# Waves of perceptron units in pairs, and outputs at the end of the same step

## The chip, the cores and the metric

The kernel runs on one core of a Trainium2 chip. The metric is the device time of one execution in microseconds (us); less is better. TensorE (PE) does matrix products into PSUM, which has eight banks of 128 partitions x 512 f32. VectorE (DVE) and ScalarE (ACT) read PSUM and write SBUF; SyncE (SP) issues nearly all DMAs; GpSimd (POOL) hardly works in the part that is changed.

## The reference

A chain of four layers on an image batch of shape (4, 16, 512, 512), f32: an attention block, a quantised 3x3 convolution with batch norm and a clip, two 3x3 convolutions with a residual, and a 3x3 convolution followed by a two-layer perceptron over the channels with a residual. The change touches the last three, as they are run in one tail loop. Cut to what matters there:

```
# layer 1
xq, wq = fake_quant(x), fake_quant(weight)
y = conv3x3(xq, wq)
y = y * inv + (beta - mean * inv)          # batch norm over the batch
x = clip(y, 0.0, 6.0)
# layer 2
out = relu(conv3x3(x, w1) + b1)
x = conv3x3(out, w2) + b2 + x
# layer 3, 128 hidden units
y = conv3x3(x, conv_w)
h = relu(einsum('bchw,kc->bkhw', y, w1) + b1)
x = x + einsum('bkhw,ck->bchw', h, w2) + b2
```

## The kernel before

The first part (attention, then a pass that takes the mean and variance for the batch norm) is left as it is. The tail is the last loop of `conv_layers`. It works through 128 tiles (`TP`), each of four image rows: 128 partitions hold rows and channels, and 2 x 512 elements lie along the free dimension. It is a pipeline in steps T. In step T each stage works on another tile:

- `load(T + 3)` (line 941): two DMAs bring the input into a buffer `tx`.
- `quantised(T + 2)`: scaling on VectorE (line 1011), rounding on ScalarE (line 1014), then four DMAs (lines 1065 and 1068) that copy quarters of `qe` into `qo`, the tile shifted by a row.
- `stage_z(T)`: the quantised convolution in bf16; each half goes out of PSUM on its own engine with the batch norm's scale and shift (line 1142 ScalarE, line 1143 VectorE), then one VectorE instruction clips both (line 1144), then four DMAs copy `ze` into `zo`.
- `stage_h(T - 1)`, `stage_x(T - 3)`, `stage_y(T - 4)`: the three f32 convolutions, each through `convolve` (line 1123), each copied out of PSUM by VectorE or ScalarE (lines 1160/1161, 1171, 1182/1183); h and x are also copied into `ho` and `xo` by four DMAs each.
- `wave(T - 6, k)` for k = 0 to 3: four matmuls of the perceptron's first layer (line 1198), one PSUM bank each; four activations into tiles `hid`, in turn on VectorE (line 1208) and ScalarE (line 1206). The function returns the four units.
- `outputs(T - 7, units)`: sixteen matmuls of the second layer over the units of four waves (line 1218), two additions on VectorE (line 1224), and one DMA to the output (line 1227).

The order of instructions on PE, DVE, ACT and SP is the order of the program; it is written out by hand (`manual_schedule`). Every DMA of the tail is in SP's order too. A wait at the head of such an order holds what is behind it.

The stages take PSUM banks from one counter: `take(n)` gives the next n of eight banks in turn. A wave takes four, every convolution two, outputs two; that is 26 in a step. A bank is written again when what it held has been read.

TensorE is split into tiles of another size by stage, which the profile prints as rows*columns: 64*32 for the convolutions, 32*128 for a wave, 128*32 for outputs. An f32 matmul shows as two records.

The kernel prepares and unpacks its arrays on the host; none of this is in the time.

Of the kernel before, what the change touches and what calls it, by code (L numbers as in the profile page):

```python
# [29 lines left out]
TP = H // 4  # L30
NH, HD = 2, 8
WS = 8
T = WS * WS
# [71 lines left out]
def conv_chain(ctx: ExitStack, tc: tile.TileContext, x, xw, mats, vecs, cqs, cws, hots, out):  # L105
# [32 lines left out]
    with tc.If(safe == 0):  # L138
        attention_block(tc, x, x1, m, v, peak)
    conv_layers(tc, x1, out, cw, cq, sw, m, v, peak)  # L140


# [784 lines left out]
def _quad(i):  # L927
    return slice(32 * i, 32 * i + 32)
# [19 lines left out]
def conv_layers(ctx: ExitStack, tc, x1, out, cw, cq, sw, m, v, peak):  # L948
# [13 lines left out]
    def take(n):  # L962
        return [banks[next(turn) % 8] for _ in range(n)]
# [3 lines left out]
    def ring(name, n, dt=F32):  # L967
        tiles = rings[name] = [
            act.tile([P, 2, WP], dt, name=f"{name}{i}") for i in range(n)
        ]  # L970
        return lambda k: tiles[k % n]
# [6 lines left out]
    ze, zo, he, ho = ring("ze", 4), ring("zo", 3), ring("he", 2), ring("ho", 2)  # L978
# [19 lines left out]
    def inner(t):  # L998
        return t[:, :, 1 : W + 1]
# [3 lines left out]
    def load(n, dst=None):  # L1003
        if dst is None:
            dst = ld.tile([P, 2, W], F32, tag="x", name=f"tx{n}")
        loaded[n] = dst
        _load_pairs(nc, dst, x1, n)
# [62 lines left out]
    def quantised(n):  # L1070
        scaled(n)
        rounded(n)
        shift(n, qe, qo, n < TP)
# [39 lines left out]
    def convolve(weights, pair):  # L1113

        p = take(2)
        for dx in range(3):
            for w in range(2):
                if pair[w] is None:
                    continue
                src, odd = pair[w]  # L1120
                for f in range(2):
                    for r in range(2):
                        nc.tensor.matmul(  # L1123
                            p[r][_quad(2 * f + w)], weights[_half(r), odd, dx, :],
                            src[_half(r), f, dx : dx + W],
                            start=dx == 0, stop=dx == 2,
                        )
        return p

    def shift_ends(n, e, o):  # L1130

        shift(n, e, o, ends=True)
        if n == TP - 1:
            for i in (0, 2):
                nc.gpsimd.memset(o(n)[_quad(i)], 0.0)

    def stage_z(n):

        if not 0 <= n < TP:
            return  # L1140
        p, z = convolve(cq, ((qe(n), 0), (qo(n), 1))), inner(ze(n))
        nc.scalar.activation(z[:, 0], p[0], AF.Identity, bias=shift_by, scale=scale)  # L1142
        nc.vector.tensor_scalar(z[:, 1], p[1], scale, shift_by, ALU.mult, ALU.add)
        nc.vector.tensor_scalar(z, z, ACT_MAX, 0.0, ALU.min, ALU.max)  # L1144
        shift_ends(n, ze, zo)

    def stage_h(n):

        if not 0 <= n <= TP:
            return  # L1150
        second = (ze(n), 0) if n < TP else None
        p, h = convolve(cw[:, 0], ((zo(n - 1), 1), second)), inner(he(n))
        if n in (0, TP):
            e = slice(n // TP, n // TP + 1)
            for f in range(2):
                nc.scalar.activation(
                    h[:, f], p[f], AF.Relu, bias=edge_b1[:, e], scale=v("edge")[:, e]
                )
        else:
            nc.scalar.activation(h[:, 0], p[0], AF.Relu, bias=v("l2_b1"))  # L1160
            nc.vector.tensor_scalar(h[:, 1], p[1], v("l2_b1"), 0.0, ALU.add, ALU.max)  # L1161
        shift(n, he, ho, n < TP)

    def stage_x(n):

        if not 0 <= n < TP:
            return
        p = convolve(cw[:, 1], ((he(n), 0), (ho(n), 1)))
        x, z = inner(xe(n)), inner(ze(n))
        for r in range(2):  # L1170
            nc.vector.scalar_tensor_tensor(
                x[:, r], p[r], v("l2_b2"), z[:, r], ALU.add, ALU.add
            )
        shift_ends(n, xe, xo)

    def stage_y(n):

        if not 0 <= n <= TP:
            return
        second = (xe(n), 0) if n < TP else None  # L1180
        p, y = convolve(cw[:, 2], ((xo(n - 1), 1), second)), inner(ye(n))
        nc.scalar.copy(y[:, 0], p[0])
        nc.vector.tensor_copy(y[:, 1], p[1])
# [5 lines left out]
    def wave(n, k):  # L1189

        if not 0 <= n < TP:
            return []
        units, p = [], take(4)
        for q in range(4):
            w, f = divmod((k + q) % 4, 2)
            par = w ^ (q % 2)
            src = ye(n + (w and not q % 2))
            nc.tensor.matmul(  # L1198
                p[q], w1[_quad(q), 1 - par, :], inner(src)[_quad(q), f, :],
                start=True, stop=True,  # L1200
            )
        for q in range(4):
            w, f = divmod((k + q) % 4, 2)
            hd = ld.tile([P, W], F32, tag="hid", name=f"hid{n}_{k}_{q}", bufs=24)
            if next(count) % 2:
                nc.scalar.activation(hd, p[q], AF.Relu, bias=v("l3_b1"))  # L1206
            else:
                nc.vector.tensor_scalar(hd, p[q], v("l3_b1"), 0.0, ALU.add, ALU.max)  # L1208
            units.append((q // 2, 2 * f + w, w ^ (q % 2), hd))
        return units  # L1210

    def outputs(n, units):

        if not units:
            return
        p, o, seen = take(2), inner(xe(n)), set()
        for r, c, par, hd in units:
            nc.tensor.matmul(  # L1218
                p[r][_quad(c)], w2[:, par], hd,
                start=(r, c) not in seen, stop=(r, c) in seen,  # L1220
            )
            seen.add((r, c))
        for r in range(2):
            nc.vector.scalar_tensor_tensor(  # L1224
                o[:, r], p[r], v("l3_b2"), o[:, r], ALU.add, ALU.add
            )
        nc.sync.dma_start(out[n], o)

    units = []
    for T in range(TP + 7):  # L1230
        if T + 3 <= TP:
            load(T + 3)
        outputs(T - 7, units)
        units = wave(T - 6, 0)
        stage_y(T - 4)
        units += wave(T - 6, 1)
        if T + 2 <= TP:
            quantised(T + 2)
        stage_x(T - 3)
        units += wave(T - 6, 2)  # L1240
        stage_h(T - 1)
        stage_z(T)
        units += wave(T - 6, 3)


def _strips(a):
# [127 lines left out]
```

## Time and profile before

| | |
|---|---|
| median of 3 runs | 5686.06 us (5681.55 to 5701.97) |
| profiled execution, its time | 5693.38 us |
| its span, first to last instruction | 5691.6 us |
| mean granted TensorE clock | 0.990 |
| busy, share of the span | PE 95%, DVE 66%, ACT 61%, POOL 12% |

The tail loop with all its stages runs from about 3586 us to the end. In the profile's 40 slices of the span, each digit the busy share of a slice in tenths, its part is the last 15 or so of each row:

```
PE   7999999999999999999999765999999999999999
DVE  4666666666666666666666555667676767676766
ACT  3777777777777777777777453444444444444444
DMA  2333233333333333333323697777767776777674
```

Durations of single instructions in the tail, mean by line: a wave's activation 743 ns on VectorE and 683 ns on ScalarE, a convolution's copy 587 to 802 ns, the clip 696 ns, the rounding 1151 ns. TensorE's records overlap (they are pipelined, several tiles at once), so for TensorE the time from the start of one piece of work to the start of the next says more than a record's duration.

### The profile page before, as it was taken

How to read it: one execution, taken by the hardware profiler on the slowest of the kernel's cores; microseconds unless marked ns; L12 is line 12 of the kernel's file. 1: busy time of each engine (PE TensorE's matmuls, PEld its weight loads, DVE VectorE, ACT ScalarE, POOL GpSimd, SP SyncE). 2: the span in 40 equal slices, each digit the busy share in tenths (PEclk: the TensorE clock that was granted, in tenths of full speed). 3: DMA queues.
4: the chain of work that ended last, by engine and by line, in shares of the span. 5: the costliest groups of instructions: out<-in, count | busy, mean ns of one | idle time of the engine just before them, and what ended most of it. 6: DMA issues, size and time to landing. Idle time of an engine off the chain costs nothing. (4 is left out here: it accounts for less than half of the span.)

```text
span 5691.6 us, 268539 instructions
## 1 busy us (share of the span) xinstructions
PE 5428.8 (95%) x120912; PEld 2891.5 (51%) x120912; DVE 3738.1 (66%) x5806; ACT 3482.3 (61%) x4739; POOL 707.5 (12%) x692
## 2 busy tenths in 40 slices
PE   7999999999999999999999765999999999999999
PEld 5666666666666666666676332322222222222222
DVE  4666666666666666666666555667676767676766
ACT  3777777777777777777777453444444444444444
POOL 1111111111111111111111352000000000000000
PEclk9999999999999999999999898999999999999999
DMA  2333333233333333333323697777767776777674
GB/s 79 77 75 74 77 71 77 65 82 71 80 73 78 73 79 73 74 77 72 81 65 60 140 247 182 173 174 176 175 174 177 174 176 173 177 175 177 173 177 107
DMA packets 626194, 677.47 MB, mean 119 GB/s; under 512 B 355856, under 2 KB 485008, under 8 KB 616848
## 3 DMA queue, kind: packets, MB, share of 16 engines
q1 hardware_dynamic: 624240, 658.76, 48.2%
q8 instruction: 953, 15.61, 1.2%
q14 instruction: 201, 1.65, 0.1%
q0 software_dynamic: 512, 1.05, 0.1%
q10 hardware_dynamic: 288, 0.39, 0.0%
HBM read 222.45 MB, written 134.48 MB: 63 GB/s over the span
## 5 line engine op out<-in xcount | busy, mean ns | idle before, releaser
L361 ACT ACTIVATE e<-pair 128x1024 f32<-128x1024 f32 x1024 | 992.8, 1022 | 449.0 <-PE pair L353 448.1
L287 PE MATMUL pair<-x,taps 32*32 32x512 f32 x18432 | 1073.8, 601 | 3.5 <-issue 2.2
L1206 ACT ACTIVATE hid<-tb,vec 128x512 f32<-128x512 f32 x1024 | 646.8, 684 | 630.7 <-PE tb L1198 630.7
L389 DVE STREAM_TRANSPOSE a<-bank 128x512 f32<-128x512 f32 x1024 | 669.9, 692 | 368.8 <-PE bank L374 354.6
L396 POOL TENSOR_TENSOR t<-a,r 128x512 f32<-128x512 f32 x512 | 542.1, 1059 | 2607.2 <-DVE r L394 2607.2
L426 ACT ACTIVATE hid<-bank,f1b 128x512 f32<-128x512 f32 x1024 | 641.4, 689 | 297.3 <-PE bank L421 233.1
L353 PE MATMUL pair<-g,y 32*128 32x128 f32 x16384 | 727.4, 287 | 50.2 <-DVE y L302 45.2
L1208 DVE TENSOR_SCALAR hid<-tb,vec 128x512 f32<-128x512 f32 x1024 | 717.9, 743 | 27.1 <-PE tb L1198 26.8
L353 PEld LDWEIGHTS pair<-g,y 32*128 32x128 f32 x16384 | 626.2, 186 | 198.1 <-issue 131.8
L421 PE MATMUL bank<-y,fc_e 32*32 32x512 f32 x8192 | 709.2, 606 | 1.0 <-DVE y L414 1.0
L374 PE MATMUL bank<-e,yt 64*32 64x128 f32 x32768 | 608.2, 274 | 28.1 <-DVE yt L346 21.0
L287 PEld LDWEIGHTS pair<-x,taps 32*32 32x32 f32 x18432 | 502.0, 103 | 182.2 <-issue 67.9
L1198 PE MATMUL tb<-ye,mat 32*128 32x512 f32 x4096 | 586.1, 639 | 0.0
L374 PEld LDWEIGHTS bank<-e,yt 64*32 64x32 f32 x32768 | 463.3, 106 | 128.3 <-issue 105.0
L1218 PE MATMUL tb<-hid,mat 128*32 128x512 f32 x4096 | 466.0, 595 | 0.0
L1123 PE MATMUL tb<-zo,cw 64*32 64x512 f32 x3096 | 365.7, 598 | 16.1 <-issue 8.9
L1123 PE MATMUL tb<-xo,cw 64*32 64x512 f32 x3096 | 361.5, 594 | 7.2 <-issue 5.3
L302 DVE TENSOR_SCALAR y<-pair,vec 128x512 f32<-128x512 f32 x128 | 90.2, 746 | 413.2 <-PE pair L287 413.2
L1123 PE MATMUL tb<-ho,cw 64*32 64x512 f32 x3072 | 357.4, 592 | 3.8 <-issue 3.0
L1123 PE MATMUL tb<-ze,cw 64*32 64x512 f32 x3072 | 360.8, 598 | 0.0
L1123 PE MATMUL tb<-he,cw 64*32 64x512 f32 x3072 | 357.7, 592 | 0.0
L1123 PE MATMUL tb<-xe,cw 64*32 64x512 f32 x3072 | 357.0, 594 | 0.0
(180 smaller groups left out, 7044.3 us busy)
## 6 DMA issues: line engine op xcount, KB each, us to landing
x<-in_xw_dram SPq DMA_DIRECT2D x64, 1320.0 KB, 5.8
zo<-ze SPq DMA_DIRECT2D x512, 128.5 KB, 2.4
ho<-he SPq DMA_DIRECT2D x512, 128.5 KB, 2.4
xo<-xe SPq DMA_DIRECT2D x512, 128.5 KB, 2.4
y<-y SPq DMA_DIRECT2D x2048, 32.0 KB, 2.6
tx<-x SPq DMA_DIRECT2D x256, 256.0 KB, 4.1
out_dram<-xe SPq DMA_DIRECT2D x128, 512.0 KB, 4.6
x<-xo SPq DMA_DIRECT2D x1008, 64.0 KB, 2.6
```

Of the source, the lines that this page charges most:

```text
L287: nc.tensor.matmul(bank(u)[quad(vv)], taps[quad(u), tap, :], xts[n][quad(u), vv, dy : dy + WS, dx : dx + BW], start=tap == 0, stop=tap == 8,)
L353: nc.tensor.matmul(bank(u)[:, P * jj : P * jj + P], y2[quad(u), vv, jl + jj].rearrange("p w t -> p (w t)"), g[quad(u), vv, jl + jj].rearra ...
L361: nc.scalar.activation(e[:, 2 * i : 2 * i + 2].rearrange("p u j t -> p u (j t)"), pairs[i], AF.Exp,)
L374: nc.tensor.matmul(bank(4 + 2 * (k % 2) + w)[quad(u), P * jj : P * jj + P], t[half, U * jj + u, w : w + 2].rearrange("p d c -> p (d c)"), ...
L389: nc.vector.transpose(a[:, 512 * w : 512 * w + 512], bank(4 + 2 * (k % 2) + w))
L396: engine.tensor_tensor(t.rearrange("p b w c -> p w b c"), top, r.unsqueeze(3).to_broadcast([P, 2, 16, C]), ALU.mult,)
L421: nc.tensor.matmul(b[quad(k)], fc1[quad(vv), quad(k)], y[quad(vv), u, :], start=True, stop=True,)
L426: nc.scalar.activation(hd, b, AF.Gelu, bias=f1b)
L1123: nc.tensor.matmul(p[r][_quad(2 * f + w)], weights[_half(r), odd, dx, :], src[_half(r), f, dx : dx + W], start=dx == 0, stop=dx == 2,)
L1198: nc.tensor.matmul(p[q], w1[_quad(q), 1 - par, :], inner(src)[_quad(q), f, :], start=True, stop=True,)
L1206: nc.scalar.activation(hd, p[q], AF.Relu, bias=v("l3_b1"))
L1208: nc.vector.tensor_scalar(hd, p[q], v("l3_b1"), 0.0, ALU.add, ALU.max)
```

## The change

The loop's order within a step is changed, and outputs are run in the step of their own waves. The loop is one step shorter. The clip of `stage_z` and the DMAs that follow it become a function of their own, called later in the step.

```diff
+
+    def capped(n):
+
+        if not 0 <= n < TP:
+            return
+        z = inner(ze(n))
         nc.vector.tensor_scalar(z, z, ACT_MAX, 0.0, ALU.min, ALU.max)
         shift_ends(n, ze, zo)
```

```diff
-    units = []
-    for T in range(TP + 7):
+    for T in range(TP + 6):
         if T + 3 <= TP:
             load(T + 3)
-        outputs(T - 7, units)
-        units = wave(T - 6, 0)
         stage_y(T - 4)
-        units += wave(T - 6, 1)
+        units = wave(T - 6, 0) + wave(T - 6, 1)
         if T + 2 <= TP:
             quantised(T + 2)
         stage_x(T - 3)
-        units += wave(T - 6, 2)
         stage_h(T - 1)
         stage_z(T)
-        units += wave(T - 6, 3)
+        units += wave(T - 6, 2) + wave(T - 6, 3)
+        capped(T)
+        outputs(T - 6, units)
```

A step before was: outputs, wave, y, wave, x, wave, h, z, wave. A step after is: y, two waves, x, h, z, two waves, outputs. The number of instructions of each kind for each tile is the same.

## The prediction

> **What bounds the kernel now.** I read the busy time in one stretch first, then the time order of one step of the tail, then the end of the chain of waits, and last the DMA queue. All rows are of core 0; times are us from the start of the span.
>
> The changed loop runs from about 3586 to the end. Busy time in 3586.10 to 5608.62 (us, then busy time and instructions of TensorE, its weight loads, VectorE, ScalarE, GpSimd, then the granted clock, DMA share, GB/s):
>
> ```profile
> 3586.10:5608.62 2022.52, 2022.52 (x28076) 604.55 (x28072) 1416.46 (x2058) 988.00 (x1451) 1.89 (x2) 1.00 0.70 174
> ```
>
> TensorE is busy throughout at the full clock (1.00); VectorE has 70% and ScalarE 49%. The two ends are starts of first waves (T=7 and T=128), so 121 steps take 2022.52: **16.715 us a step**, all of it TensorE's pitch. What counts is what each piece of a step costs TensorE from its start to the next start. Time order (start, duration, engine, line, tiles, merged count):
>
> ```profile
> 4505.43 1.14 PE L1198 MATMUL tb<-ye,mat 32*128 32x512 f32 x8
> 4506.50 0.63 PE L1123 MATMUL tb<-xo,cw 64*32 64x512 f32 x4
> ...
> 4508.70 0.61 PE L1123 MATMUL tb<-xe,cw 64*32 64x512 f32 x4
> 4509.24 1.14 PE L1198 MATMUL tb<-ye,mat 32*128 32x512 f32 x8
> 4510.31 0.63 PE L1123 MATMUL tb<-he,cw 64*32 64x512 f32 x4
> ...
> 4513.05 1.14 PE L1198 MATMUL tb<-ye,mat 32*128 32x512 f32 x8
> 4514.12 0.63 PE L1123 MATMUL tb<-zo,cw 64*32 64x512 f32 x4
> ...
> 4516.72 0.40 PE L1123 MATMUL tb<-qe,cq 64*32 64x512 bf16 x4
> ...
> 4517.51 1.14 PE L1198 MATMUL tb<-ye,mat 32*128 32x512 f32 x8
> 4518.58 3.64 PE L1218 MATMUL tb<-hid,mat 128*32 128x512 f32 x32
> 4522.15 1.14 PE L1198 MATMUL tb<-ye,mat 32*128 32x512 f32 x8
> ```
>
> Start to start: a wave 1.07, an f32 convolution before a wave 2.74, h before z 2.60, z before a wave 0.79, outputs 3.57. Four waves, y, x, h, z and outputs give 4x1.07 + 2x2.74 + 2.60 + 0.79 + 3.57 = 16.72, the step. Inside a piece f32 groups follow at 0.43; where the tile size changes (64*32, 32*128, 128*32) the next starts 0.54 after the last group, so **a change costs 0.11**. A wave is two groups, 0.86; its first four loads are spread over another 0.10, and 0.11 is its exit: 1.07.
>
> **What the merged order saves.** Before there are eight changes of tile size, after it five. By pieces:
> - Two waves together: 1.07 + 0.86 = 1.93 instead of 2.14; 0.21 saved, twice.
> - x goes straight into h: 2.60 (as h into z), not 2.74; 0.14 saved. h then begins without a change of size; its first group's extra 0.03 goes, 2.57.
> - Outputs go into y, 128*32 to 64*32, which no row of before shows. The ends: 3.46 if nothing drains, 3.57 as outputs into a wave. The Trainium skill, "TensorEngine Tiling (Array Packing)", Key Properties, says that a change of tiling mode drains the array, whichever the sizes. All changes seen here cost the same, so I take 3.57; 3.46 would be 0.11 x 121 = 13 us more gain.
>
> Without waits: 2.74 + 1.93 + 2.60 + 2.57 + 0.79 + 1.93 + 3.57 = 16.13, or **0.59 saved**.
>
> **What it pays: the eight PSUM banks.** A step takes 26 banks in turn, before and after, and a bank is free when the use eight takes earlier has been copied out. A double wave takes all eight. In the new order the second wave of y's pair reuses the banks of outputs and y, that of z's pair the banks of h and z; x's first banks are those of the pair's first two units. The end of before, where no convolution stands between waves, shows what this costs. From the chain of waits (start, us):
>
> ```profile
> 5658.47 3.68 PE tb L1198 x24
> ```
>
> and the copies of the same stretch on VectorE:
>
> ```profile
> 5658.67 0.69 DVE L1183 COPY ye<-tb 128x512 f32<-128x512 f32 x1 [1.20 <-PE tb L1123]
> 5659.56 4.04 DVE L1208 TENSOR_SCALAR hid<-tb,vec 128x512 f32<-128x512 f32 x6 [0.20 <-PE tb L1198]
> ```
>
> Three waves take 3.69 (5658.40 to 5662.09) and not 1.07 + 2x0.86 = 2.79. The first wave starts at s = 5658.40; y's VectorE copy ends at s+0.96 and the first unit's copy starts at s+1.16. The third wave's third unit needs the bank of VectorE's second unit, done at s+1.16+1.41 = s+2.57. With 0.13 from copy to matmul, and 0.97 from a delayed last unit to the next piece (0.43 + 0.54), that is s+3.67; seen 3.69. This gives me the waits of the change:
> - y's pair: y's copy ends at s+0.96, so the second wave's last unit starts at s+1.09 and x at s+2.06. x's own banks are free at s+1.16+0.74+0.13 = s+2.03 (VectorE) and, by ScalarE, 0.04 later: s+2.07. Natural was 1.93: **0.14 lost**.
> - z's pair: z's VectorE half (row below) ends at 4518.59, 1.08 after its wave, and the second wave's last unit starts at 1.21, outputs at 2.18 to 2.19: **0.26 lost**. Outputs' own banks are free at 2.08, and the last wave's activations end at 1.16 + 2.72 (four in a row, another row of the end) = 3.9, while outputs reach them at 2.19 + 2.58 = 4.77. No wait there.
>
> ```profile
> 4517.79 0.80 DVE L1143 TENSOR_SCALAR ze<-tb,scale,shift 128x512 f32<-128x512 f32 x1
> 4518.69 0.70 DVE L1144 TENSOR_SCALAR ze<-ze 128x1024 f32<-128x1024 f32 x1
> ```
>
> So the step is 16.13 + 0.14 + 0.26 = **16.53, 0.185 less**.
>
> A rule speaks against the whole change: the same page's PSUM Bottleneck section warns that packed matmuls leave the copies out of PSUM as the bound. If TensorE had to wait for all eight copies, each pair would last 1.16 + 2.72 + 0.13 = 4.0, 2.1 over 1.93, and the step would be 3.6 longer, 440 us in all. The row weighs more: only reused banks hold a matmul, and here these are the oldest two.
>
> **Moved work.** The clip (0.70, VectorE) goes behind four activations: it ends 3.9 + 0.7 = 4.6 after the pair's start. Behind it on VectorE stand outputs' additions, which are ready only at 2.19 + 3.72 = 5.9, so it costs them nothing. zo's four DMAs wait for it, but SP is still issuing ho then (2.4 for four, behind xo). The output DMA is now ahead of the loads on SP: it waits for the additions until 1.57 after y's start, while zo is still issuing until 2.5. `capped` adds no instruction.
>
> **SP and xo.** y of the next step needs xo, the DMAs behind qo, which wait for the rounding on ScalarE. These rows are before:
>
> ```profile
> 4512.51 1.15 ACT L1014 ACTIVATE qe<-tx,unround 128x1024 bf16<-128x1024 f32 x1 [0.74 <-DVE tx L1011]
> ...
> 4517.94 1.23 SPq L1068 DMA_DIRECT2D xo<-xe  x2
> ```
>
> and of tile xo
>
> ```profile
> DMA to landing us min/median/max: 2.3/2.4/4.4
> ```
>
> Rounding ends at 4513.66; the last xo is issued at 4518.55 and lands after 2.4 at 4520.95, 7.3 after the rounding (in some steps SP slips by up to 1). y starts at 4523.22: 2.3 to spare. After: the pair starts 2.74 after y, its four VectorE copies and the scaling push the rounding's end to 8.5 after y (7.2 before). xo lands at 15.8, the slipped ones at 16.8, against 16.53. Mostly hidden, with 0.7 to spare; I charge 0.03 a step.
>
> **Ends.** The ramp loses about 1: the first wave stood beside a wait of 2.59 for xo at 3568.62 and no longer does. The drain: before, from 5608.62 to the end of outputs, 77.0. After, by the same pieces: 15.8, 16.2 and 13.8 for T=128 to 130 (pairs of 2.1 to 2.7), 11.3 twice (y, four waves at 5.0, outputs), 8.9: 77.3. The dropped step saves nothing; its outputs move up.
>
> **Sum.** 121 x (0.185 - 0.03) = 18.8 less, 1 given back: **18 us**. The profiled execution took 5693.4 (span 5691.6), so 5675; it lay 7.3 over the median, so against 5686.06 the forecast is **5668**, 0.3% faster. A measurement of this kernel tells some 0.5% (28 us) from no change; the forecast is within that.
>
> **Rivals.**
> - *The banks hold up less than I think.* If neither pair waited: 0.59 x 121 = 71 less, 5615. For it: copies could end sooner, outputs may enter y without a drain. Against: the end of before waits as worked out. To pass 28 us the step need only save 0.24, so a third of the waits less, or the missing drain (18 + 13 = 31), is enough: 5655. Chance 0.30.
> - *xo becomes the bound (slower).* Place: y's first matmul, waiting for the last xo DMA. If the landing slips to 4.4, the row's maximum, in most steps, xo lands at 8.5 + 4.9 + 4.4 = 17.8, and the step is 17.8: 1.1 longer, 5815. It decides from 16.53 + 0.19 = 16.72; it is slower by over 28 us from a mean of 16.95, 1.1 later than the usual 15.8. For it: SP is issuing some 13 of 16.5 us, and the spare time falls from 2.3 to 0.7. Against: the median of 2.4 with the same DMAs in flight. Half-way, 5720. Chance 0.22.
> - *Waits of xo eat just the gain*: 5680 to 5700, within 0.5%. It is part of no change. With my forecast, chance 0.48.
>
> **Range.** 5640 (no drain into y, waits of 0.25 in place of 0.40) to 5698 (landings slipped in half of the steps). The forecast's own is 5658 to 5680. Faster 0.30, same 0.48, slower 0.22.
>
> **What would show it.** Right: TensorE's pitch near 16.5; in a step, two stretches of 16 wave records with the next piece 2.07 and 2.19 after their start; x into h at 2.60; outputs into y at 3.57. Wrong: a y that starts over 3.6 after outputs with the xo DMA as releaser; outputs that wait for activations of the last wave; a pair of 1.93; a slower granted clock.

## The result and the profile after

The changed kernel took 5675.88 us (median of 22 runs, 5648.74 to 5686.48) against 5686.48 before (22 runs beside it, 5662.19 to 5701.97): a ratio of **0.9979, 95% interval 0.9967 to 0.9992**. By the ratio that is about 12 us less. It is clear of zero with 22 runs of each, and smaller than the 0.5% below which the prediction speaks of no change. The profiled execution has a span of 5677.1 instead of 5691.6, 14.5 less.

Busy time of the changed kernel between the starts of T=7's and T=128's first pair of waves (columns as in the prediction):

```profile
3587.33:5596.28 2008.95, 2008.88 (x28081) 770.99 (x28073) 1416.18 (x2058) 965.22 (x1451) 1.89 (x2) 1.00 0.72 176
```

TensorE is still busy all the time at the full clock. The same 121 steps now take 2008.95: **16.603 us a step, 0.112 less than 16.715**, which is 13.6 of the 14.5 us. In this execution the first outputs also came 1.5 earlier (at 3581.0 instead of 3582.5). That can't be credited to the change: nearly all of what lies ahead of them is the same program in every run, and in the recorded executions they come anywhere from 3552 to 3587. The end of the loop gives 0.6 back.

One step after, in order of time on TensorE (line 1204 is a wave, 1224 outputs; x reads `he` and `ho`, h reads `zo` and `ze`):

```profile
4500.23 2.14 PE L1204 MATMUL tb<-ye,mat 32*128 32x512 f32 x16
4502.29 0.63 PE L1123 MATMUL tb<-he,cw 64*32 64x512 f32 x4
...
4504.90 0.61 PE L1123 MATMUL tb<-zo,cw 64*32 64x512 f32 x4
...
4507.47 0.39 PE L1123 MATMUL tb<-qe,cq 64*32 64x512 bf16 x4
...
4508.28 2.23 PE L1204 MATMUL tb<-ye,mat 32*128 32x512 f32 x16
4510.44 3.64 PE L1224 MATMUL tb<-hid,mat 128*32 128x512 f32 x32
4514.01 0.63 PE L1123 MATMUL tb<-xo,cw 64*32 64x512 f32 x4
...
4516.75 2.14 PE L1204 MATMUL tb<-ye,mat 32*128 32x512 f32 x16
```

The two pairs cost 2.06 and 2.16 from start to start, x into h 2.61, outputs into y 3.57. This step has 16.52; the mean is longer mostly because y is, by 0.03 to 0.72 in 27 of 120 steps. The wait list of the changed kernel between 3600 and 5580 has a line with xo as releaser that before didn't have (total us, times, longest):

```profile
PEld tb L1123 <- DMA xo<-xe: 17.7, 26, 0.9
```

and this is such a step, first TensorE's matmuls, then its weight loads with the idle time before them:

```profile
5276.08 1.35 PE L1123 MATMUL tb<-xo,cw 64*32 64x512 f32 x5
5276.83 0.64 PE L1123 MATMUL tb<-xe,cw 64*32 64x512 f32 x4
...
5279.54 0.71 PE L1204 MATMUL tb<-ye,mat 32*128 32x512 f32 x4
```

```profile
5276.08 0.14 PEld L1123 LDWEIGHTS tb<-xo,cw 64*32 64x32 f32 x2 [0.84 <-DMA ho<-he]
5276.81 0.12 PEld L1123 LDWEIGHTS tb<-xo,cw 64*32 64x32 f32 x3 [0.59 <-DMA xo<-xe]
```

y begins on time with the rows of xo that are there; the next one is held for 0.59 until xo's last DMA lands, and y takes 3.46 instead of 2.74. (0.84 of idle weight loading is usual at a change of tile size; it is no loss.)

### The profile page after: what moved, and what is told of

It reads as the page before. It is cut to its first block, busy times and chain, and to the rows that moved or that the text cites. A ratio compares the mean times of both kernels' runs of the same rounds, so it can differ in the third digit from the quotient of the medians.

```text
span 5677.1 us, 268907 instructions
## 1 busy us (share of the span) xinstructions
PE 5416.8 (95%) x120912; PEld 3061.6 (54%) x120912; DVE 3738.3 (66%) x5806; ACT 3460.0 (61%) x4739; POOL 707.3 (12%) x692
## 5 line engine op out<-in xcount | busy, mean ns | idle before, releaser
L1214 DVE TENSOR_SCALAR hid<-tb,vec 128x512 f32<-128x512 f32 x1024 | 697.7, 744 | 39.9 <-PE tb L1204 27.4
L1212 ACT ACTIVATE hid<-tb,vec 128x512 f32<-128x512 f32 x1024 | 620.3, 689 | 111.1 <-PE tb L1204 111.1
L1204 PE MATMUL tb<-ye,mat 32*128 32x512 f32 x4096 | 564.0, 622 | 0.0
L1188 ACT COPY ye<-tb 128x512 f32<-128x512 f32 x129 | 75.8, 587 | 657.5 <-PE tb L1123 657.5
L1204 PEld LDWEIGHTS tb<-ye,mat 32*128 32x128 f32 x4096 | 255.7, 183 | 260.6 <-issue 218.0
```

Of the source, the lines that this page charges most:

```text
L1204: nc.tensor.matmul(p[q], w1[_quad(q), 1 - par, :], inner(src)[_quad(q), f, :], start=True, stop=True,)
```

## The experiments

All edits are against the changed kernel unless said otherwise. "z then h" in a name means that z stands ahead of h. This table is worked out from the starts of TensorE's matmul records in one traced execution of each kernel: the mean, over some 119 steps between 3600 and 5580, of the time from the first record of a piece to the first of the next. "x, h, z" runs from the start of x to the start of the pair; "(single)" means that the waves stand one by one (1.07 each); the 5.000 of "four waves" is all four. The last column is the time of all runs against the kernel before.

| kernel | y | pair behind y | x, h, z | pair before outputs | step | ratio, interval |
|---|---|---|---|---|---|---|
| before | 2.737 | (single) | (single) | (single) | 16.715 | 1 |
| the change | 2.798 | 2.072 | 5.990 | 2.170 | 16.599 | 0.9979 (0.9967 to 0.9992) |
| clip first | 2.737 | 2.068 | 5.986 | 2.590 | 16.952 | 1.0058 (1.0038 to 1.0079) |
| first pair only | 2.753 | 2.007 | (single) | (single) | 16.695 | 1.0003 (0.9991 to 1.0016) |
| second pair only | 2.737 | (single) | 5.961 | 2.137 | 16.556 | 0.9962 (0.9938 to 0.9985) |
| four waves | (into x) | | | 5.000 | 17.108 | 1.0072 (1.0045 to 1.0099) |
| relabelled | 2.737 | (single) | (single) | (single) | 16.723 | 0.9995 (0.9984 to 1.0006) |
| xo first | 2.737 | 2.078 | 6.109 | 2.137 | 16.633 | 0.9977 (0.9967 to 0.9986) |
| half of z | 2.806 | 2.071 | 5.993 | 2.000 | 16.441 | one run |
| xo first, z then h | 2.737 | 2.079 | 6.106 | 2.066 | 16.560 | 0.9963 (0.9950 to 0.9976) |
| xo and ho first, z then h | 2.737 | 2.078 | 6.003 | 2.095 | 16.484 | 0.9933 (0.9912 to 0.9954) |
| second pair only, z then h | 2.737 | (single) | 5.960 | 2.122 | 16.540 | 0.9964 (0.9948 to 0.9979) |
| z then h | 2.799 | 2.071 | 5.995 | 2.095 | 16.535 | 0.9968 (0.9951 to 0.9984) |

The step column can tell 0.01 us (1 us in all); the ratios can't tell less than some 10 us, since a kernel's runs differ by half a per cent.

**The order alone, without pairs.** Is the gain that of the dropped step or of the clip's place?

```diff
+        units = wave(T - 6, 0)
         stage_y(T - 4)
-        units = wave(T - 6, 0) + wave(T - 6, 1)
+        units += wave(T - 6, 1)
...
         stage_x(T - 3)
+        units += wave(T - 6, 2)
         stage_h(T - 1)
         stage_z(T)
-        units += wave(T - 6, 2) + wave(T - 6, 3)
+        units += wave(T - 6, 3)
         capped(T)
         outputs(T - 6, units)
```

> Order of the stages as before (every wave alone), but outputs in the step of their own waves, one step fewer, and the clip behind the last wave's activations. My account: TensorE's cycle of pieces is the same as before, so 16.72 us a step and no change within 0.2%. Rival (the change's gain comes from the step that is dropped, or from the clip's later place): the whole 12 to 14 us of the change, 16.6 us a step.

Measured: 16.723 and 0.9995. The dropped step and the later clip bring nothing by themselves; before too, outputs followed the last wave directly, only under the next T. The gain comes with taking the single waves out of their places.

**One pair at a time.** First pair only: the last two waves stay apart.

```diff
         stage_x(T - 3)
+        units += wave(T - 6, 2)
         stage_h(T - 1)
         stage_z(T)
-        units += wave(T - 6, 2) + wave(T - 6, 3)
+        units += wave(T - 6, 3)
```

> Only the pair behind y is joined; the waves around x, h and z are one by one as before. My account by pieces: y 2.74, pair 2.07, x 2.74, wave 1.07, h 2.60, z 0.79, wave 1.07, outputs 3.57 = 16.65, with a little wait for xo at y 16.67; 0.05 to 0.07 less than before, 5 to 8 us less: about 5680. Rival (two waves cost 1.93, the gain of the change is in both pairs alike and the rest is lost elsewhere): 16.5.

Measured: 16.695, only 0.02 less than before, where 0.05 to 0.07 was expected. The pair behind y and x together cost 2.007 + 2.834 = 4.84, where 2.07 + 2.74 = 4.81 was expected. In order of time on TensorE:

```profile
4510.86 0.63 PE L1123 MATMUL tb<-he,cw 64*32 64x512 f32 x4
4510.98 0.63 PE L1123 MATMUL tb<-ho,cw 64*32 64x512 f32 x4
```

x starts earlier, but its second group comes 0.12 behind the first and not 0.03, and TensorE pays for that at the next change of tile size. In 117 of 118 steps a wait instruction for a further DMA semaphore stands between x's first weight loads; two runs below have the same fault in another place. y's wait for xo adds 0.016. So in this order the pair is worth next to nothing; how much of that is the wait instruction was not tested.

Second pair only: waves ahead of and behind y stay single.

```diff
+        units = wave(T - 6, 0)
         stage_y(T - 4)
-        units = wave(T - 6, 0) + wave(T - 6, 1)
+        units += wave(T - 6, 1)
```

> Only the pair behind z is joined, x runs straight into h; waves ahead of and behind y stay single. My account: outputs 3.57, wave 1.07, y 2.74, wave 1.07, x 2.60, h 2.58, z 0.79 to 0.81, pair 2.16 = 16.58 to 16.60, and no wait for xo, since the rounding is as early as before: 14 to 16 us less than before, about 5671, so as good as or better than the whole change. Rival (the two pairs bring the same): half of the change's gain, 5681.

Measured: 16.556, 0.159 less than before, and no wait for xo. **This half of the change alone is better in its step than the whole**; the intervals of the ratios, 0.9962 and 0.9979, overlap and can't show it. The rival, two pairs of equal worth, falls.

**What bounds a row of waves.** All four together:

```diff
         stage_y(T - 4)
-        units = wave(T - 6, 0) + wave(T - 6, 1)
...
-        units += wave(T - 6, 2) + wave(T - 6, 3)
+        units = sum((wave(T - 6, k) for k in range(4)), [])
         capped(T)
```

> y, x, h, z in one row, then all four waves together, then outputs: three changes of tile size a step. By bank reuse: the third and fourth wave wait for the copies of the first and second, as at the end of the kernel before (four waves in 5.0 to 5.3): 2.60 + 2.58 + 2.58 + 0.81 + 5.0 + 3.57 = 17.1 us a step, about 50 us slower than before, 5735. Rival (changes of tile size are what costs, copies keep up): four waves in 1.07 + 3 x 0.86 = 3.65, a step of 15.8, 5575.

In order of time on TensorE:

```profile
4505.59 5.07 PE L1204 MATMUL tb<-ye,mat 32*128 32x512 f32 x32
4510.58 3.64 PE L1224 MATMUL tb<-hid,mat 128*32 128x512 f32 x32
```

and from its wait list between 3650 and 5580, the waves' weight loads waiting for the copies of earlier units:

```profile
PEld tb L1204 <- DVE hid L1214: 178.1, 450, 0.5
```

The four waves take 4.99 and not 3.65: from the third on, every unit needs the bank of a unit two waves earlier, and the copies set the pace. What two changes of tile size fewer save is lost several times over; the kernel is slower than before. With pairs the copies go on beside the next piece: those of the pair at 4508.28 in the step shown above run on VectorE until 4512.17, while outputs start at 4510.44.

**The clip ahead of the pair.**

```diff
         stage_z(T)
+        capped(T)
         units += wave(T - 6, 2) + wave(T - 6, 3)
-        capped(T)
         outputs(T - 6, units)
```

> The changed kernel, but with the clip of z and zo's DMAs back at once behind z's copies, ahead of the pair's activations on VectorE. My account: outputs' first PSUM bank is that of the pair's first unit, whose VectorE copy now starts at 1.79 after the pair (behind the clip) and not at 1.16, so outputs start at 1.79 + 0.74 + 0.13 = 2.66 instead of 2.16; the step grows by 0.50 to about 17.1 us, 60 us in all: 5735, slower than before by some 0.8%. Rival (VectorE has 30% to spare, so the place of a 0.70 us clip doesn't matter): a step of 16.6 and 5676.

VectorE in this kernel, then TensorE:

```profile
4505.29 0.69 DVE L1150 TENSOR_SCALAR ze<-ze 128x1024 f32<-128x1024 f32 x1
4505.90 2.72 DVE L1214 TENSOR_SCALAR hid<-tb,vec 128x512 f32<-128x512 f32 x4
```

```profile
4504.12 2.24 PE L1204 MATMUL tb<-ye,mat 32*128 32x512 f32 x16
4506.70 3.64 PE L1224 MATMUL tb<-hid,mat 128*32 128x512 f32 x32 [0.34 <-DVE hid L1214]
```

The activations start 1.78 after the pair, as expected, and outputs wait for the first of them: 4505.90 + 0.74 = 4506.64, and outputs start at 4506.70. The pair costs 2.59 and the kernel is slower than before (1.0058). The size was off: 0.42 more a pair, not 0.50, because from the copy's end to the matmul it is 0.06 here and not 0.13; and y no longer waits for xo, which gives 0.06 back. Where the clip stands decides whether the change gains or loses, on an engine with 30% to spare.

**Half of z's copy left out.**

```diff
-        nc.vector.tensor_scalar(z[:, 1], p[1], scale, shift_by, ALU.mult, ALU.add)
+        nc.vector.tensor_scalar(
+            z[:, 1, 0 : W // 2], p[1][:, 0 : W // 2], scale, shift_by, ALU.mult, ALU.add
+        )
```

(`ze` is also cleared once ahead of the loop.)

> The changed kernel, but VectorE copies only the first 256 columns of its half of z (the others are left out). My account: z's bank comes free some 0.3 earlier, so it no longer holds the pair's last unit; but outputs' own first bank is that of the pair's first unit, free at about 2.05, so the pair costs 2.05 to 2.08 instead of 2.16, 10 to 13 us in all, and not the 1.93 of two waves with no wait. Rival (z's copy is the only wait there): 1.93, 28 us.

```profile
4509.52 2.06 PE L1208 MATMUL tb<-ye,mat 32*128 32x512 f32 x16
4511.51 3.64 PE L1228 MATMUL tb<-hid,mat 128*32 128x512 f32 x32
```

```profile
4509.77 0.53 DVE L1145 TENSOR_SCALAR ze<-tb,scale,shift 128x256 f32<-128x256 f32 x1
```

z's VectorE copy takes 0.53 instead of 0.80, and the pair costs 1.99 (2.000 in the mean): below the 2.05 that I gave for the banks of outputs, above the 1.93 of the rival. So z's VectorE copy is the wait of this pair, worth 0.17 of the 0.24 over 1.93. What stands next is not the banks of outputs, as I had expected. This kernel's wait list between 3650 and 5580 has, for the pair's weight loads,

```profile
PEld tb L1208 <- ACT ze L1144: 23.7, 115, 0.2
```

that is the other half of z, which ScalarE copies: the second wave's third unit waits for it in nearly every step. Outputs' first bank is free just before they start: the copy of the pair's first unit ends 1.91 after the pair's start.

**xo's DMAs ahead of qo's.**

```diff
 def quantised(n):
     scaled(n)
     rounded(n)
-    shift(n, qe, qo, n < TP)
...
         stage_x(T - 3)
+        if T + 2 <= TP:
+            shift(T + 2, qe, qo, T + 2 < TP)
         stage_h(T - 1)
```

(The two calls of `quantised` ahead of the loop are each followed by their `shift`.)

> The changed kernel with the four DMAs of qo issued behind xo's and no longer ahead of them. My account: y's matmuls no longer meet xo's last DMAs; y costs 2.74 in the mean and not 2.80, the step 16.54 and not 16.60, 7 us less than the changed kernel in all. Rival (the longer y is not a wait for xo but for something else, such as the weight loads behind outputs): y stays at 2.80.

Measured: y is at 2.737 and waits no more, so the longer y was the wait for xo. But the step is 16.633, not the 16.54 expected, and longer than with the change: x, h and z cost 0.12 more. The next run has the same fault and shows where it is.

**z ahead of h, with xo first.**

```diff
         stage_x(T - 3)
-        stage_h(T - 1)
+        if T + 2 <= TP:
+            shift(T + 2, qe, qo, T + 2 < TP)
         stage_z(T)
+        stage_h(T - 1)
```

> As with xo's DMAs ahead of qo's, and z ahead of h, so that h stands before the pair. My account: z's copies are long done when the pair starts, and h's copy on VectorE no longer queues behind another one; the pair costs 2.05 to 2.12 and not 2.16, z then h 0.65 + 2.71 and not 2.58 + 0.81; a step of about 16.43, some 35 us less than before, 20 less than the changed kernel. Rival (copies of an f32 convolution come no earlier than z's, since both are read when TensorE has finished): the pair stays at 2.16, a step of 16.5.

The pair is at 2.066, as expected: the VectorE copy that it waits for, now h's, ends 0.96 after its start, where z's ended at 1.06 with the change. But h before it costs 2.857 and not 2.71, so the step is 16.560 and not 16.43. TensorE in this kernel, x's first groups and z's last:

```profile
4513.23 0.63 PE L1123 MATMUL tb<-he,cw 64*32 64x512 f32 x4
4513.28 0.75 PE L1123 MATMUL tb<-ho,cw 64*32 64x512 f32 x4
...
4516.05 0.40 PE L1123 MATMUL tb<-qe,cq 64*32 64x512 bf16 x4
4516.07 0.54 PE L1123 MATMUL tb<-qo,cq 64*32 64x512 bf16 x4
```

One of the four ho matmuls is late, so the group of four spans 0.75 instead of 0.63, and the lag stays in every later group (0.54 instead of 0.40) up to the next change of tile size. The trace shows one instruction more there, in this kernel and the one before: the second ho matmul of x waits for two DMA semaphores, and a wait instruction of 0.051 stands ahead of its weight load. Here that is so in 117 of 120 steps, and in each of them this matmul starts 0.125 or more behind the first; with the change it has one wait in every step and starts 0.007 behind. The data isn't late: in the step shown, the later of the two DMAs had landed 2.4 us before. DMAs take eight semaphores in turn, so the order of their issue decides which waits a matmul needs; with the change, by my reading, y's wait for xo had already covered the other one. The next order is built to have one wait there.

**qo's DMAs behind ho's as well.**

```diff
         stage_x(T - 3)
-        if T + 2 <= TP:
-            shift(T + 2, qe, qo, T + 2 < TP)
         stage_z(T)
         stage_h(T - 1)
+        if T + 2 <= TP:
+            shift(T + 2, qe, qo, T + 2 < TP)
```

(against the kernel of the section above)

> As the kernel with xo's DMAs first and z ahead of h, but qo's DMAs now behind ho's too. What I found in the run before: with qo's DMAs between xo's and ho's, the second ho matmul of x waits for two DMA semaphores and not one, an extra wait instruction ahead of its weight load, which puts it 0.12 behind its group; the lag stays until the next change of tile size, so h before the pair costs 2.86. In this order the second wait is not in the program. My account: h before the pair back at 2.71 to 2.74, all else the same, a step of 16.43, 35 us less than before. Rival (the lag is one of the PSUM banks or of ho's data coming late): h stays at 2.86, a step of 16.56.

The same place of this kernel:

```profile
4522.77 0.63 PE L1123 MATMUL tb<-he,cw 64*32 64x512 f32 x4
4522.82 0.63 PE L1123 MATMUL tb<-ho,cw 64*32 64x512 f32 x4
...
4525.59 0.40 PE L1123 MATMUL tb<-qe,cq 64*32 64x512 bf16 x4
4525.62 0.42 PE L1123 MATMUL tb<-qo,cq 64*32 64x512 bf16 x4
```

The group is whole again, with one wait and 0.007 between the first two ho matmuls in every step, and h costs 2.753: the lag went with the second wait. The pair is 2.095, not 2.06, so the step is 16.484, not 16.43. Its time is 5643.94 (median of 6), **0.9933 (0.9912 to 0.9954)**: faster than both kernels, its interval clear of the change's.

**z ahead of h, alone and with the second pair only.**

```diff
         stage_x(T - 3)
-        stage_h(T - 1)
         stage_z(T)
+        stage_h(T - 1)
```

> The changed kernel with z ahead of h and nothing else. My account: the pair at 2.06 in place of 2.16, h before the pair at 2.74, y still with its wait for xo (2.80 in the mean): 16.49 a step, 27 us less than before, 13 less than the changed kernel. Rival (the wait for xo grows by what the pair gains, since the DMAs set the pace there): y at 2.90, a step of 16.59 as with the change.

> Only the pair behind the convolutions is joined, and z stands ahead of h. My account: as the kernel with only that pair (16.56), with the pair at 2.06 in place of 2.14: 16.48 a step, 28 us less than before, no wait for xo.

Measured: 16.535 and 16.540, each some 0.05 longer than expected. The swap takes 0.075 off the pair of the whole change and y stays at 2.799, so the rival falls: a shorter step doesn't lengthen the wait for xo one for one. With the second pair alone the swap gains 0.015 only (2.122, not 2.06). Its pair is longer than the 2.095 of the other kernel, but h ahead of it is shorter by as much: h and pair together cost 4.83 and 4.84.

## Why the prediction was right, point by point

The forecast was 5668 and no measurable change; measured 5675.88, a ratio of 0.9979 where 5668 stood for 0.9968. "No change" alone proves little, since it covers any difference under 28 us; the terms of the sum say more:

- *Changes of tile size, 0.59 without waits.* What can be read of it is right. x into h is 2.60, h into z 2.575, and outputs into y 3.573: this change of size, which before didn't show, costs what the others cost. The 1.93 of two waves without a wait is seen nowhere; the shortest pair of any run in this stretch is 1.98.
- *Pair behind y, 2.07.* 2.072. The sum was right; its parts weren't. In the step shown above, the delayed unit starts 0.05 after y's copy ends, not 0.13, but its second record follows 0.53 after its first and not 0.43: some 0.10 of weight load shows anew. The prediction had tried only the sum of the two, 1.10 from copy to next piece, on a row of before, so the errors cancel here; where one of them counted alone, with the clip first, they didn't.
- *Pair behind z, 2.18 to 2.19.* 2.170. That z's VectorE copy holds it is shown by the halved copy. Next comes ScalarE's half of z, not outputs' own banks.
- *Clip free where it is now.* Right, and shown by its opposite. VectorE after:

```profile
4508.54 0.80 DVE L1143 TENSOR_SCALAR ze<-tb,scale,shift 128x512 f32<-128x512 f32 x1
4509.44 2.73 DVE L1214 TENSOR_SCALAR hid<-tb,vec 128x512 f32<-128x512 f32 x4
4512.09 0.69 DVE L1150 TENSOR_SCALAR ze<-ze 128x1024 f32<-128x1024 f32 x1
4514.16 1.41 DVE L1230 SCALAR_TENSOR_TENSOR xe<-tb,vec,xe 128x512 f32<-128x512 f32 x2 [1.39 <-PE tb L1224]
```

  The four activations start 1.16 after the pair at 4508.28; the clip is done at 4512.78 and outputs' additions wait for TensorE until 4514.16, 1.39 of idle time.
- *xo mostly hidden, 0.03 a step.* The mechanism was right, the term too small: y is 0.061 longer in the mean, twice what I charged. 0.031 x 121 is 3.7 us of the gain that I counted and that isn't there.
- *z before the pair, 0.79.* 0.815. I left this out: x's second group starts 0.052 behind its first (median) and not 0.027, and as x, h and z now run without a change of tile size between them, the lag is paid once, at the pair. Another 0.025 a step, 3 us. Why the group is late isn't shown; in this kernel a wait instruction for a DMA stands ahead of x's first weight load, but x also follows a pair for the first time.
- *Ends: 1 lost.* From the first outputs to the last the loop takes 2089.5 instead of 2102.5, 13.0 less, of which the 121 steps give 13.6. So some 0.6 was lost there. From the start of y of T=128 to the end of outputs it takes 77.6, where 77.3 was forecast. What the ramp ahead of the first outputs lost can't be told from the executions' own differences.

Together: 0.155 a step forecast, 0.112 measured, 18.8 and 13.6 us. Of the rivals, xo as the bound (slower) is real as a wait but far from its point of decision; banks that hold up less than thought didn't come; and xo's waits ate 0.061 a step, a third of the 0.185 and not all of it. The reckoning in which a pair waits for all eight copies, 4.0 us, is far from both pairs.

The same working says where the gain lies. x and h cost 0.161 less than before, because x runs straight into h. The two pairs cost 4.242 where four single waves cost 4.286, so only 0.044 less. y, z and outputs give 0.093 back.

## What to carry to other kernels

Where TensorE is the bound, count each change of tile size and each wait at its own place, start to start. Here a change costs 0.11 us. Joining two waves spares 0.21 by that count, and waiting for its own PSUM banks costs a pair 0.14 to 0.24, so the joining itself nearly cancels; most of what is gained is that the convolutions stand together where the waves were taken out. Before joining work, look when the copies of the banks that it reuses end, and keep work that nobody waits for (the clip) behind the copies that TensorE waits for. When a step gets shorter, look at what was late by little before: most of what this gain fell short by is a DMA that had 2.3 us to spare and then had less than none in 27 of 120 steps.

## What was not expected of the hardware

A single late matmul in a group that runs side by side isn't caught up: the lag of 0.12 went through three convolutions (x, h and z 6.109 instead of 5.990) and was paid at the next change of tile size. In the three kernels in which a wait instruction stands between the weight loads of a group (first pair only, xo first, and xo first with z then h), such a lag goes with it, and in the step looked at what it waits for had landed 2.4 us before. Which DMA falls to which semaphore, and so the order of DMA issues on SP, decides whether it is there (h before the pair at 2.857 or 2.753 with the same work). And the wait for a copy costs more than the time until the copy ends: the delayed wave shows 0.10 of weight load again.
